# A third tile for the states of the scans, and DRAM rows 36 KB apart

## The chip, the cores and the metric

The kernel runs on one core of one Trainium2 chip. A core has five engines with instruction queues of their own: TensorE (PE, with weight loads PEld beside it) for matmuls, VectorE (DVE) for elementwise work, reductions and scans, ScalarE (ACT) for activation functions and copies, GpSimd (POOL) for elementwise work, and SyncE (SP), which here issues nearly all DMAs. Each engine works through its queue in order; semaphores hold an instruction back until what it needs is there. SBUF is the core's working memory, PSUM the memory that TensorE writes, and DRAM is reached by DMAs, which 16 DMA engines carry out. The metric is the device time of one execution in microseconds.

## The reference, cut to what matters

The input is 16 images of 192 channels on a 32 x 32 grid (L = 1024 positions). Four layers follow each other: an mLSTM block with a 3 x 3 convolution and a batch norm, a channel attention with depthwise convolutions, a two-dimensional selective scan, and a block that mixes rolled copies of the image. The change concerns the third layer (and two small tiles of the second). Its heart, per image, for 4 directions k, 384 channels d and 16 states n:

```python
def step(h, xs_t):
    d_t, u_t, B_t, C_t = xs_t
    dA = jnp.exp(d_t[..., None] * A)
    h = h * dA + (d_t * u_t)[..., None] * B_t[:, :, None, :]
    y = jnp.einsum('bkdn,bkn->bkd', h, C_t)
    return (h, y)
_, ys = jax.lax.scan(step, h0, (dT, uT, BT, CT))
```

The steps d_t are a softplus of a projection of the layer's input; directions 2 and 3 run backwards, and directions 1 and 3 run over the transposed grid.

## The kernel before, in words

All arithmetic is in float32. The first layer runs for all images first, in a loop, and takes about the first 3500 us. Then class `LayersB` does the other three, image by image: `prepare` (second layer and the input side of the third), `scans` (the recurrence), `complete` (the output side of the third layer and the fourth). While image b is scanned, `prepare` of image b+1 and `complete` of image b-1 are woven in.

*Units.* A unit is a scan of one tile of 128 partitions: 16 channels times 8 states, 1024 positions long. Two units (blocks of states 0 to 7 and 8 to 15) make a group, 24 groups a direction, 4 directions an image: 192 units an image, 3072 in all. For each unit:

- ScalarE (`decay`, L1835) makes dA = exp(A x dl) into a ring of three tiles. dl holds the steps of the group's 16 channels, each row repeated on 8 partitions.
- ScalarE (`inputs_up`, L1831), once per group, copies du (step times input, repeated likewise) into one of two PSUM tiles xt.
- VectorE (`inputs`, L1842) multiplies it by the B states bb; both multiplies of a group stand ahead of its two scans.
- VectorE (`scan`, L1851) runs the recurrence over dA and xt into a tile h. There are two h tiles, taken in turn.
- POOL (`outputs`, L1863) multiplies h by the C states cb into hc, a ring of three.
- TensorE (`sums`, L1893) adds over the states with four matmuls into the PSUM tile acc; ScalarE (`collect`, L1903) copies acc out once in four units.

*Steps.* `front` makes the steps of a direction, small pieces at fixed slots: a projection (TensorE), then for each of six halves `ends` (ScalarE: Abs into the tile e, Relu into dlh), `logs` (ScalarE: e = exp(-e), e = ln(1 + e)), and `park` two slots later (L1769; POOL: dlh + e into dlh, dlh times x into duh). `park` stores dlh and duh in the DRAM tiles dld and dud, a row of 1024 positions per channel. Successive halves are six slots apart. `keep` stores the B and C rows in xdr.

*Loads.* `load_group` (L1793) reads 16 rows of dld and of dud, each onto 8 partitions, into a ring of two tiles each; it is issued as soon as the decay that reads the old tile has been put in the queue, three groups ahead. `load_states` (L1789) reads 8 rows of xdr, the whole set 16 times over, into bb and cb. All these go through SP's queue, in which each issue waits its turn.

*Order.* In `scans` the order of all engines' queues is written by the kernel itself, unit by unit (a slot each): decays, scans, products, sums and loads have fixed places, and the pieces of `prepare` and `complete` are put in by `fits` and `advance`, which keep a reckoned clock per engine (constants SLOT, OWN, OVER, LEAST) and ask whether an engine has room before the slot's end. Semaphore waits follow from which instructions touch the same tile. Elementwise and TensorE instructions of the woven-in stages are recorded through one helper and all carry the line L782.

*Small tiles of `prepare`.* kk holds the diagonal of the key products; m1 and m2 hold the two matrices that attention leaves. They lie in a pool of small tiles under the tags m1 and m2. Larger tiles lie in slots that are reused in turn: "pa" (one buffer: x0, later x1) and "w" (two buffers, for weights).

Of the kernel before, what the change touches and what calls it, by code (L numbers as in the profile page):

```python
# [11 lines left out]
F32 = mybir.dt.float32  # L12
# [7 lines left out]
C, H, W = 192, 32, 32  # L20
L = H * W
HL = L // 2
P6 = 96
# [4 lines left out]
K, N, R = 4, 16, 12  # L28
# [13 lines left out]
class Ctx:  # L42
# [22 lines left out]
    def ln_exp(self):  # L65
# [4 lines left out]
        if self.ordered:  # L70
            self.spent["ACT"] += TABLE
        i = self.nc.scalar.preload_act_table_set("natural_log_exp_and_others")
# [672 lines left out]
BLOCKS = N // NBL  # L745
# [10 lines left out]
ENGINES = ("PE", "ACT", "POOL", "DVE")  # L756
ALLOW = {"PE": 2.45, "DVE": 0.3}
OVER = {"PE": (0.8, 1.2), "ACT": (0.0, 1.5), "POOL": (0.5, 1.5)}
LEAST = {"PE": 1.0, "ACT": 0.6, "POOL": 0.8}
TABLE = 1.28  # L760
MARGIN = 0.6


class Metered:


    RATES = {"ACT": (0.07, 0.00105), "POOL": (0.1, 0.0022), "DVE": (0.08, 0.00105), "PE": (0.06, 0.0017)}
    LEAST = {"ACT": 0.2, "POOL": 0.2, "DVE": 0.12, "PE": 0.4}

# [3 lines left out]
    def __getattr__(self, op):  # L773
        f = getattr(self.engine, op)

        def issue(out, *args, **kw):
            base, each = self.RATES[self.name]
            self.spent[self.name] += max(self.LEAST[self.name], base + each * math.prod(out.shape[1:]))
            if op == "activation" and args[1] in (AF.Tanh, AF.Gelu):
                self.spent["ACT"] += TABLE * self.cx.has_ln  # L780
                self.cx.has_ln = False
# [15 lines left out]
class Stream:  # L797
# [16 lines left out]
    def inputs(self):  # L814


        done, engine = self.dones[-3 if self.piped else -1]
        return 0.0 if engine == self.engine else done + MARGIN

# [5 lines left out]
class LayersB:  # L825
# [81 lines left out]
    def setup(self):  # L907

        tc, nc, cx, wp, I, NB = self.tc, self.nc, self.cx, self.wp, self.I, self.NB
        dp = self.dp  # L910
        self.dqd = dp.tile([6, 128, 9, 128], F32, name="dqd")
        self.dvd = dp.tile([2, 2, P6, 9, P6], F32, name="dvd")
        self.vd = dp.tile([P6, 2, L], F32, name="vd")
        self.x0d = dp.tile([P6, 2, L], F32, name="x0d")
        self.x2d = dp.tile([P6, 2, L], F32, name="x2d")
        self.xdr = dp.tile([K, 2 * N, L], F32, name="xdr")
        self.dld = dp.tile([K, 3, 128, L], F32, name="dld")
        self.dud = dp.tile([K, 3, 128, L], F32, name="dud")
        self.xxd = dp.tile([3, 128, L], F32, name="xxd")
        self.yd = dp.tile([3, 128, L], F32, name="yd")  # L920
        self.zd = dp.tile([NB, 3, 128, L], F32, name="zd")
        self.x1d = dp.tile([NB, P6, 2, L], F32, name="x1d")


        bn_g, bn_b = self.vec("bn_g", P6), self.vec("bn_b", P6)
        self.bsc = wp.tile([P6, 2], F32, name="bsc")
        self.bsh = wp.tile([P6, 2], F32, name="bsh")
        with tc.tile_pool(name="b_pre0", bufs=1) as pre:
            st = pre.tile([P6, 2, NB, 12], F32, name="st")
            for a in range(2):  # L930
                nc.scalar.dma_start(
                    st[:, a], self.sdram[:, a * P6 : (a + 1) * P6, :].rearrange("b p s -> p b s")
                )
            mv = pre.tile([P6, 2, 2], F32, name="mv")
            for a in range(2):
                nc.vector.bn_aggr(mv[:, a, :], st[:, a].rearrange("p b s -> p (b s)"))
            sd = pre.tile([P6, 2], F32, name="sd")
            nc.scalar.activation(sd, mv[:, :, 1], AF.Sqrt, bias=cx.eps5[0:P6])
            nc.vector.reciprocal(sd, sd)
            nc.vector.tensor_mul(self.bsc, sd, bn_g)  # L940
            nc.vector.tensor_mul(sd, mv[:, :, 0], self.bsc)
            nc.vector.tensor_sub(self.bsh, bn_b, sd)


        self.offb = wp.tile([P6, P6], F32, name="offb")
        nc.sync.dma_start(self.offb, I["c_off48"])
        self.temp = wp.tile([P6, 2], F32, name="temp")
        for a in range(2):
            for j in range(2):
                nc.sync.dma_start(  # L950
                    self.temp[48 * j : 48 * j + 48, a : a + 1],
                    I["temperature"][2 * a + j : 2 * a + j + 1].unsqueeze(0).to_broadcast([48, 1]),
                )

        self.dw2b = self.vec("dw_b", 128)
        self.pads = [wp.tile([128, H + 2, W + 2], F32, name="pad%d" % i) for i in range(2)]
        for t in self.pads:
            nc.gpsimd.memset(t, 0.0)

        self.xx = wp.tile([128, 3, L], F32, name="xx")  # L960
    def setup_scans(self):

        nc, cx, wp, I = self.nc, self.cx, self.wp, self.I
# [50 lines left out]

        ring = lambda name, n, shape: [wp.tile(shape, F32, name=name + str(i)) for i in range(n)]
        self.y = wp.tile([128, 3, L], F32, name="y")
        self.dA, self.h, self.hc = ring("dA", 3, [128, L]), ring("h", 2, [128, L]), ring("hc", 3, [128, L])
        self.dl, self.du = ring("dl", 2, [128, L]), ring("du", 2, [128, L])
        self.bb, self.cb = ring("bb", BLOCKS, [128, L]), ring("cb", 3, [128, L])
        self.e, self.dlh, self.duh = (wp.tile([128, HL], F32, name=n) for n in ("e", "dlh", "duh"))  # L1020
        self.xd = wp.tile([64 + XR, L], F32, name="xd")
        self.dtw = wp.tile([64 + R, INNER], F32, name="dtw")
        self.xt = [self.xp.tile([128, L], F32, name="xt%d" % i) for i in range(2)]
# [108 lines left out]
    def prepare(self, b):  # L1132

        nc, cx, sm, I = self.be, self.cx, self.sm, self.I
# [42 lines left out]
        for m in range(3):  # L1177
# [5 lines left out]
            elif m == 1:  # L1183
                w1 = self.weight(self.w1d, [P6, 2, C])
            else:
                wpf = self.weight(I["w_projfT"].rearrange("(a p) o -> p a o", p=P6), [P6, 2, C])
# [13 lines left out]

        id6 = cx.ident[0:P6, 0:P6]
        at = sm.tile([P6, 2, P6], F32, tag="at", name="at", bufs=1)
        kk = sm.tile([P6, 2, C], F32, tag="m1", name="kk", bufs=1)[:, :, 0:P6]
        rq = sm.tile([P6, 2], F32, tag="rq", name="rq")
        vs = [self.p4([P6, 2, HL], "vh") for _ in range(2)]
        for hf in range(2):
# [19 lines left out]
        for a in range(2):  # L1226
# [5 lines left out]
                nc, pk[:, ch(a)], [(qT[:, t, k0 : k0 + P6], qT[:, t, k0 : k0 + P6]) for t in range(NCH)]  # L1232
            )
        yield "DVE", 0
        nc.vector.tensor_mul(
            kk, pk.rearrange("p (a c) -> p a c", a=2), id6.unsqueeze(1).to_broadcast([P6, 2, P6])
        )
# [34 lines left out]
        yield "ACT", 0  # L1272
        for a in range(2):
            nc.scalar.mul(at[:, a, :], at[:, a, :], den[:, a : a + 1])
        m1 = sm.tile([P6, 2, C], F32, tag="m1", name="m1", bufs=1)
        m2 = sm.tile([P6, 2, C], F32, tag="m2", name="m2", bufs=1)
        for m_, w_ in ((m1, w1), (m2, wpf)):
            yield "PE", 0
            p = self.mm()[0:P6, 0 : 2 * C]
            for a in range(2):  # L1280
                nc.tensor.matmul(p[:, a * C : (a + 1) * C], lhsT=at[:, a, :], rhs=w_[:, a, :], start=True, stop=True)
            yield "ACT", 0
            nc.scalar.copy(m_, p.rearrange("p (a c) -> p a c", a=2))
        ds = [self.taps(P6, self.dvd[1, 0], I["dw_kv"][ch(0)], b == 0)]
        for hf in range(2):
            for a in range(2):
# [400 lines left out]
    def fits(self, s, end):  # L1687

        if not s.open(self.slots) or s.engine == "SP":
            return s.engine == "SP" and s.open(self.slots)  # L1690
        at = self.clock[s.engine]
        if s.engine != "DVE":
            end += OVER[s.engine][self.slots % BLOCKS]
        wait = s.inputs()
        if wait > at and (s.engine == "DVE" or wait + LEAST[s.engine] > end):
            return False
        return at < end + 0.1 and self.have.get(s.engine, 1.0) > 0.0

# [145 lines left out]
    def scan(self, u):  # L1844
        nc = self.nc
        n, blk = divmod(u, BLOCKS)
        k = n // GROUPS
        views = [self.h[u % 2], self.dA[u % 3], self.xt[(n + 1 + blk) % 2]]
        if k >= 2:
            views = [v[:, ::-1] for v in views]  # L1850
        nc.vector.tensor_tensor_scan(*views, 0.0, op0=ALU.mult, op1=ALU.add)  # L1851

    def outputs(self, u, carried=False):

        n, blk = divmod(u, BLOCKS)

        k = n // GROUPS - K * (carried and u == UNITS - 1)
        views = [self.hc[u % 3], self.h[u % 2], self.c_of(k, blk)]
        if n // GROUPS % 2:
            views = [views[0].rearrange("p (h w) -> p w h", w=W)] + [  # L1860
                v.rearrange("p (w h) -> p w h", h=H) for v in views[1:]
            ]
        self.nc.gpsimd.tensor_mul(*views)  # L1863
# [139 lines left out]
```

## Time and profile before

| what | value |
|---|---|
| median of 3 runs | 15609.16 us (15584.52 to 15626.19) |
| the profiled execution | 15591.93 us, of which the span 15590.1 us |
| busy, share of the span | PE 81%, DVE 79%, POOL 63%, ACT 59% |
| scans, L1851 | 3072 x 2273 ns |
| products with C, L1863 | 3072 x 2371 ns |
| multiplies with B, L1842 | 3072 x 1227 ns |
| decays, L1835 | 3072 x 1146 ns |
| copies of u, L1831 | 1536 x 1014 ns |
| dl and du loads | 2 x 1536 of 512 KB |
| read from DRAM, written | 2018.92 MB, 364.30 MB |

A busy share is the time in which an engine executed something, as a share of the span. A row of the waits view names who waited, for whom, the sum of the idle time, the number of times and the longest. A row of the groups view gives line, engine, operation, tiles, shapes and number, then busy time and mean, then the engine's idle time ahead of these instructions with what ended most of it. The stretches view gives each engine's busy time between two points of the execution, with the clock that TensorE was granted, the busy share of the DMA engines and the rate at which they moved data.

### The profile page before, as it was taken

What the parts mean: (1) busy time and instruction counts of PE and PEld (TensorE: products, weight loads), DVE (VectorE), ACT (ScalarE), POOL (GpSimd) and SP (SyncE); (2) the same over time, 40 slices, a digit from 0 to 9 for tenths busy, and PEclk for the clock granted to TensorE, in tenths of its full rate; (3) what the DMA queues carried; (4) which work ended last, traced back from release to release, by engine and by line L of the source; (5) the groups of instructions that cost most, each with busy time, mean ns of one, the idle gap of its engine ahead of it and who ended that gap; (6) DMA issues with size and microseconds to landing.
All of it is one profiled execution on the core that took longest, in us unless ns stands there. A gap on an engine that the chain in (4) does not pass through costs nothing. (4 is left out here: it accounts for less than half of the span.)

```text
span 15590.1 us, 196674 instructions
## 1 busy us (share of the span) xinstructions
PE 12621.5 (81%) x72384; PEld 5045.6 (32%) x72384; DVE 12310.8 (79%) x10295; ACT 9263.9 (59%) x12084; POOL 9861.8 (63%) x5787
## 2 busy tenths in 40 slices
PE   9999999987787777877787777877787777878755
PEld 5555555542222222222222222222222222222212
DVE  4444444448988999999989898898989898988997
ACT  3333333326666666666666666666666666666665
POOL 1000000006787878787878787878878787878785
PEclk9999999997787888878788888887888887878766
DMA  1000000017777787878787878787777787777775
GB/s 29 12 15 14 15 14 15 15 40 189 201 195 200 188 207 188 210 182 214 182 211 183 213 184 211 183 210 189 202 194 198 194 202 195 199 195 193 201 182 129
DMA packets 852126, 2412.70 MB, mean 155 GB/s; under 512 B 114352, under 2 KB 234240, under 8 KB 843520
## 3 DMA queue, kind: packets, MB, share of 16 engines
q1 hardware_dynamic: 838496, 2397.64, 60.2%
q8 instruction: 580, 9.50, 0.3%
q10 hardware_dynamic: 12704, 2.72, 0.1%
q14 instruction: 346, 2.83, 0.1%
HBM read 2018.92 MB, written 364.30 MB: 153 GB/s over the span
## 5 line engine op out<-in xcount | busy, mean ns | idle before, releaser
L1863 POOL TENSOR_TENSOR hc<-h,cb 128x1024 f32<-128x1024 f32 x3072 | 7247.3, 2371 | 2046.2 <-DVE h L1851 1557.8
L1851 DVE TENSOR_TENSOR_SCAN h<-dA,xt 128x1024 f32<-128x1024 f32 x3072 | 6912.8, 2273 | 297.0 <-POOL hc L1863 289.1
L1842 DVE TENSOR_TENSOR xt<-xt,bb 128x1024 f32<-128x1024 f32 x3072 | 3633.4, 1227 | 852.7 <-ACT xt L1831 718.9
L1835 ACT ACTIVATE dA<-dl,A 128x1024 f32<-128x1024 f32 x3072 | 3506.7, 1146 | 801.2 <-DMA dl<-dld 672.8
L1893 PE MATMUL acc<-hc,sel 128*32 128x256 f32 x24576 | 2406.8, 473 | 1707.6 <-POOL hc L1863 1705.0
L782 PE MATMUL mm<-pad,dg 128*128 128x512 f32 (+1 forms) x5580 | 2899.3, 655 | 13.3 <-ACT pad L782 9.9
L1831 ACT COPY xt<-du 128x1024 f32<-128x1024 f32 x1536 | 1557.6, 1014 | 1361.7 <-DVE h L1851 1183.5
L1893 PEld LDWEIGHTS acc<-hc,sel 128*32 128x32 f32 x24576 | 562.2, 120 | 4055.4 <-POOL hc L1863 2897.2
L782 PEld LDWEIGHTS mm<-pad,dg 128*128 128x128 f32 (+1 forms) x5580 | 995.5, 192 | 1479.2 <-issue 1363.3
L596 POOL TENSOR_TENSOR vw<-va,gtok 128x396 f32<-128x396 f32 x112 | 95.2, 850 | 1712.0 <-ACT va L588 1712.0
L782 PE MATMUL mm<-x,wgt 96*128 96x512 f32 (+1 forms) x1664 | 1064.5, 775 | 140.1 <-ACT o L782 50.0
L1884 PE MATMUL acc<-y,ident 128*128 128x512 f32 x576 | 445.7, 866 | 445.5 <-ACT y L1903 444.5
L782 POOL TENSOR_TENSOR t<-x 96x768 f32<-96x768 f32 (+4 forms) x510 | 647.5, 1290 | 204.6 <-PE mm L782 204.2
L691 POOL TENSOR_TENSOR x_in<-x_in,sz 128x384 f32<-128x384 f32 x128 | 116.8, 913 | 750.5 <-DVE x_in L687 676.7
L782 PE MATMUL mm<-d,xT 128*96 128x256 f32 x2048 | 569.1, 416 | 5.6 <-ACT o L782 5.3
L782 PEld LDWEIGHTS mm<-x,wgt 96*128 96x128 f32 (+1 forms) x1664 | 342.1, 226 | 669.9 <-issue 364.5
L782 POOL TENSOR_TENSOR duh<-dlh,xx 128x512 f32<-128x512 f32 x384 | 537.5, 1400 | 30.1
L782 POOL TENSOR_TENSOR dlh<-dlh,e 128x512 f32<-128x512 f32 x384 | 488.4, 1272 | 103.1 <-ACT e L782 101.2
L782 PE MATMUL mm<-xd,dtw 12*128 12x512 f32 x768 | 534.5, 782 | 10.0 <-ACT z L782 10.0
L622 DVE TENSOR_TENSOR D<-D,s 128x256 f32<-128x256 f32 x768 | 270.8, 415 | 322.6 <-ACT D L619 322.6
L389 PE MATMUL pc<-ypad,w_c 128*64 128x512 f32 (+1 forms) x1152 | 442.9, 633 | 80.4 <-PEq L735 41.3
L619 ACT ACTIVATE D<-s 128x256 f32<-128x256 f32 x768 | 232.7, 390 | 426.3 <-PE s L613 426.3
(331 smaller groups left out, 15374.9 us busy)
## 6 DMA issues: line engine op xcount, KB each, us to landing
dl<-dld SPq DMA_DIRECT2D x1536, 512.0 KB
du<-dud SPq DMA_DIRECT2D x1536, 512.0 KB
dld<-dlh SPq DMA_DIRECT2D x384, 256.0 KB
dud<-duh SPq DMA_DIRECT2D x384, 256.0 KB
bb<-xdr SPq DMA_DIRECT2D x128, 512.0 KB
cb<-xdr SPq DMA_DIRECT2D x128, 512.0 KB
dg<-dqd SPq DMA_DIRECT2D x270, 192.0 KB
zd<-z SPq DMA_DIRECT2D x48, 512.0 KB
```

Of the source, the lines that this page charges most:

```text
L389: nc.tensor.matmul(p[r, :], lhsT=w_, rhs=v, start=(n == 0), stop=(n == 14))
L619: nc.scalar.activation(d, S[j][:, two], AF.Exp)
L622: nc.vector.tensor_mul(d, d, S[j][:, 2 * CH :])
L691: nc.gpsimd.tensor_mul(hT[:, :, cs], hT[:, :, cs], sz[:, :, cs])
L782: return f(out, *args, **kw)
L1831: self.nc.scalar.copy(self.xt[n], self.du[n])
L1835: self.nc.scalar.activation(self.dA[u % 3], self.dl[n % 2], AF.Exp, scale=self.A[:, blk, n : n + 1])
L1842: self.nc.vector.tensor_mul(self.xt[(n + 1 + blk) % 2], self.xt[n % 2], self.bb[blk])
L1851: nc.vector.tensor_tensor_scan(*views, 0.0, op0=ALU.mult, op1=ALU.add)
L1863: self.nc.gpsimd.tensor_mul(*views)
L1884: nc.tensor.matmul(acc, lhsT=self.cx.ident, rhs=self.y[:, g, half(pair)], start=True, stop=False)
L1893: nc.tensor.matmul(self.acc[rows4(q), q4(s)], lhsT=self.sel[:, m, :], rhs=self.hc[u % 3][:, q4(q)], start=False, stop=(s + m + blk == 3),)
```

## The change

The ring of h tiles has three instead of two, and the scan and the product take tile u % 3. The memory comes from three places: the tile e is no longer a tile of its own but another name of duh; kk takes the slot "pa" between x0 and x1; m1 and m2 take buffers of the slot "w". The DRAM tiles xdr, dld and dud get a dimension of 9 of which only place 0 is used, so that their rows, still 4 KB long, lie 36 KB apart. LEAST becomes a pair per engine, read by the slot's block, and both numbers of each pair are the old one.

```diff
-LEAST = {"PE": 1.0, "ACT": 0.6, "POOL": 0.8}
+LEAST = {"PE": (1.0, 1.0), "ACT": (0.6, 0.6), "POOL": (0.8, 0.8)}
+PITCH = 9
...
-        self.xdr = dp.tile([K, 2 * N, L], F32, name="xdr")
-        self.dld = dp.tile([K, 3, 128, L], F32, name="dld")
-        self.dud = dp.tile([K, 3, 128, L], F32, name="dud")
+        self.xdr = dp.tile([K, 2 * N, PITCH, L], F32, name="xdr")[:, :, 0, :]
+        self.dld = dp.tile([K, 3, 128, PITCH, L], F32, name="dld")[:, :, :, 0, :]
+        self.dud = dp.tile([K, 3, 128, PITCH, L], F32, name="dud")[:, :, :, 0, :]
...
-        self.dA, self.h, self.hc = ring("dA", 3, [128, L]), ring("h", 2, [128, L]), ring("hc", 3, [128, L])
+        self.dA, self.h, self.hc = ring("dA", 3, [128, L]), ring("h", 3, [128, L]), ring("hc", 3, [128, L])
...
-        self.e, self.dlh, self.duh = (wp.tile([128, HL], F32, name=n) for n in ("e", "dlh", "duh"))
+        self.dlh, self.duh = (wp.tile([128, HL], F32, name=n) for n in ("dlh", "duh"))
+        self.e = self.duh
...
-        kk = sm.tile([P6, 2, C], F32, tag="m1", name="kk", bufs=1)[:, :, 0:P6]
...
+        kk = self.slot("pa", [P6, 2, P6], "kk")
...
-        m1 = sm.tile([P6, 2, C], F32, tag="m1", name="m1", bufs=1)
-        m2 = sm.tile([P6, 2, C], F32, tag="m2", name="m2", bufs=1)
-        for m_, w_ in ((m1, w1), (m2, wpf)):
+        ms = []
+        for w_ in (w1, wpf):
...
+            m_ = self.slot("w", [P6, 2, C], "m", 2)
+            ms.append(m_)
             nc.scalar.copy(m_, p.rearrange("p (a c) -> p a c", a=2))
+        m1, m2 = ms
...
-        if wait > at and (s.engine == "DVE" or wait + LEAST[s.engine] > end):
+        if wait > at and (s.engine == "DVE" or wait + LEAST[s.engine][self.slots % BLOCKS] > end):
...
-        views = [self.h[u % 2], self.dA[u % 3], self.xt[(n + 1 + blk) % 2]]
+        views = [self.h[u % 3], self.dA[u % 3], self.xt[(n + 1 + blk) % 2]]
...
-        views = [self.hc[u % 3], self.h[u % 2], self.c_of(k, blk)]
+        views = [self.hc[u % 3], self.h[u % 3], self.c_of(k, blk)]
```

## The prediction

> **What bounds the kernel now.** I read the busy shares first, then the stage in which the change works, cut out of the trace, then each engine's waits in that stage. The scans run from about 3530 us to 15460 us; the slices of the page show the busy shares jump there.
>
> The stretches view, with busy time of each engine, then granted clock, DMA share and GB/s. Rows 1 and 2 are the two halves of one plain load (xx, no row read twice; row 2 runs on into a plain store), row 3 is dl, du and cb loads, row 4 a plain y load, and the last row is the whole scan stage:
>
> ```profile
> 7150.40:7153.20 2.80, 2.80 (x13) 0.97 (x12) 2.70 (x4) 1.86 (x2) 2.80 (x4) 0.72 1.02 250
> 7153.40:7157.20 3.80, 3.31 (x18) 1.39 (x17) 3.80 (x2) 0.00 (x0) 3.80 (x5) 1.00 1.02 412
> 5537.20:5541.30 4.10, 4.10 (x19) 1.86 (x18) 4.10 (x2) 1.94 (x2) 4.02 (x4) 1.00 1.00 226
> 5693.00:5694.80 1.80, 1.80 (x12) 0.57 (x11) 1.70 (x2) 1.77 (x3) 1.80 (x1) 1.00 1.01 239
> 3530.00:15460.00 11930.00, 9204.18 (x42540) 3207.12 (x42538) 10738.50 (x7134) 7896.12 (x9521) 9531.36 (x5248) 0.80 0.77 196
> ```
>
> In the last row the columns are PE, PEld, DVE, ACT, POOL. VectorE is busy 10738.5 of 11930 us (90%), POOL 80%, PE 77%, ACT 66%, the DMA engines 77%. VectorE sets the pace: 3072 units at 11930/3072 = 3.88 us each, of which its two large operations take 2.27 + 1.23 us. Only its 1191 us of idle time can be won. The waits view of the scan stage says what ends them (VectorE, then ScalarE; us in total, times, longest):
>
> ```profile
> DVE xt L1842 <- ACT xt L1831: 718.9, 356, 29.7
> DVE h L1851 <- POOL hc L1863: 289.1, 229, 3.3
> ```
>
> ```profile
> ACT xt L1831 <- DVE h L1851: 1183.5, 563, 4.4
> ACT dA L1835 <- DMA dl<-dld: 672.8, 239, 7.7
> ```
>
> The second row is what a third state tile addresses: a scan that cannot start because the product of two units ago still reads its tile. The first is larger, and is ScalarE being late with the copy of u. The last row is one cause of that lateness, a replicated load not yet landed, and is what the row pitch could address. The groups view gives durations:
>
> ```profile
> L1863 POOL TENSOR_TENSOR hc<-h,cb 128x1024 f32<-128x1024 f32 x3072 | 7247.3, 2371 | 2046.2 <-DVE h L1851 1557.8
> L1851 DVE TENSOR_TENSOR_SCAN h<-dA,xt 128x1024 f32<-128x1024 f32 x3072 | 6912.8, 2273 | 297.0 <-POOL hc L1863 289.1
> ```
>
> POOL's 2.37 us fits easily in 3.88, so it is late only when other work sits in front: 1.27 + 1.40 us for the two step products, up to 1.9 us for one roll product. Such a lump is caught up later (POOL itself waits 1557.8 us for scans).
>
> **What the Trainium skill says.** "SBUF — State Buffer", section "SBUF: two separate sides": VectorE and GpSimd share a port pair under an exclusive lock, against a GpSimd read when the VectorE operation has two SBUF inputs. More overlap of scan and product could then stretch both. Here scan and multiply each read one operand from PSUM, and the trace agrees that they are free: the 3072 scans last 2241/2276/2290 ns (least/median/most) with POOL busy 80% of the time. "DMA: Bandwidth & Descriptors", section "Latency and other measured facts", gives row pitches of 512 KiB and more as slow and a few KiB of padding as the cure; neither 4 KB nor 36 KB is such a pitch, so it promises nothing either way, and no run here shows those pitches. The same page's "Where 436 GB/s comes from" puts the ceiling at 435 GB/s; the 412 of row 2 above is near it; row 3, of replicated loads, has 226, and the plain loads of rows 1 and 4 have 250 and 239.
>
> **The change, part by part.**
>
> *Order.* Built, both programs hold the same instructions in the same order on TensorE, VectorE and GpSimd. ScalarE and SP differ only around the first image, before the order is fixed by hand. The pairs in LEAST carry the old values twice. So only waits and addresses change: 0 us from instructions.
>
> *Third h tile.* The scan of unit u now waits for the product of u-3. The longest of the 229 waits is 3.3 us and one unit of slack is 3.88 us, so I count all 289 us as removed at their place. How much stays won? I followed each such wait in the trace to VectorE's next wait for ScalarE. Counting gaps over 50 ns (282 of them, 295 us), for 155 us ScalarE was itself found waiting for VectorE in between, so its work moves forward too and the gain passes. For the other 140 us the late copy comes first, and ScalarE was held by TensorE or a load. These follow VectorE only through the products and decays; I keep 30%, 42 us. Ends: nothing of the 140, or all of it. Taken: 155 + 42 = 197 us, between 155 and 289.
>
> *New lateness.* With three tiles POOL may fall one unit further behind. What is late next is the sum of that unit (L1893), then ScalarE's collect (L1903), once in four units, behind which the next copy of u is queued. 229/4 = 57 cases of 1.26 us is 72 us on ScalarE, which is idle a third of the time; I charge 10 us, 0 to 72.
>
> *e inside duh.* ScalarE's Abs now waits until the previous duh has been stored. In the trace that store lands a median of 4.9 us before the next Abs starts, 0.28 us at the 5th percentile; in the scans 9 are late, by some 4 us together. Behind a late Abs stand the next decay and copy. Cost 4 us; if all 88 cases with under 2 us of room slipped by 2 us, 176 us on ScalarE. What covers it is the three units between one store and the next Abs.
>
> *kk and the m tiles.* kk waits for readers of x0 that are long done. The in_proj weight load must now wait for the attention matmuls just before it, with the next dl and du issues behind it on SP, 15 times. SP there waits for ScalarE's decays anyway (4415 us in its own waits). 5 us, at most 15 x 4 = 60.
>
> *Row pitch.* dl and du rows, and the states' rows, go from 4 KB to 36 KB apart; packets and bytes stay. From the packet records, matched to the issues in order, a 4 KB packet takes 255 ns in a dl load, 280 in du, 261 in cb and 271 in bb, and 159 at best. So there is something to win, but the rows' place does not look like the cause. The patterns have 16 outer steps, and I read them as one step for each of 16 engines: then in cb and bb all engines go through the same eight rows, in dl and du through sixteen different ones, and the times are alike. Plain loads are as slow: y takes 275 ns, x0d 569 for 8 KB against 309 at best. And a dl load that starts on idle queues runs its second to fourth packets per engine at 166 to 206 ns, and the fifth to eighth, of the same rows, at 262 to 324. I take 0 us. Ends: at 159 ns the loads' share of the DMA engines falls from 0.59 to 0.36 and the DMA waits mostly go; of the 719 us, 269 came with ScalarE held by a load within 9 us before (mixed causes included), so up to -269 us. The other end is below as a rival.
>
> **Sum.** -197 + 10 + 4 + 5 = about -180 us against the profiled execution's own 15591.9 us (span 15590.1, 1.8 around it): 15412. The median of the three runs, 15609.2, lies 17 us above that execution, so 15430, 1.2% faster.
>
> **Rivals.**
> 1. *The pitch helps as well.* For it: 672.8 us of load waits, loads at 60% of the best rate. Against: the unreplicated loads just cited. Half to all of 269 us more: 15160 to 15300.
> 2. *The wait only moves.* TensorE is late in the largest group of ScalarE's delays (153 of my count of 411 late copies, 253 us, with nothing else holding ScalarE). If it does not follow VectorE, and POOL's extra lag delays its sums, then only about 40 us stay: 15570, within 0.3%.
> 3. *The pitch hurts, slower.* The replicated loads hold 0.59 of the DMA engines (8 packets per engine x 255 to 280 ns x 3296 loads, 7050 us of 11930), the rest 0.18. Place: load after load behind SP, then the decay L1835. Packets 10% longer land a pair 0.43 us later, 245 x 0.43 = 105 us on ScalarE and 40% of it, 42 us, on VectorE; these grow with new late loads. The gain is spent near packets 1.35 times as long; from (1-0.18)/0.59 = 1.39 times the DMA engines are the bound. At 1.5 times the stage is 11930 x (0.59 x 1.5 + 0.18) = 12700 us: 16380. For it: already 77% busy. Against: nothing shows packets slower on wider rows.
>
> **How the numbers follow.** Forecast 0.50, own range 15350 to 15520. Rival 1: 0.24. Rival 2: 0.14. Rival 3: 0.12. A measurement here tells 0.3% (47 us) from no change. Faster: the first two, with a little given to no change, 0.73; same 0.15; slower 0.12. The range runs from 15120 to 15650: it leaves out rival 3 and the far end of rival 1.
>
> **What would show it.** Right: VectorE's wait for hc at the scan falls from 289 to under 30 us; VectorE's wait for ScalarE's copy grows, by 50 to 130 us; the busy time of VectorE stays within 10 us; dl packets stay at 240 to 270 ns and the load waits at 600 to 800 us. ScalarE's first operation into duh waits under 30 us for the store. The prediction is wrong if the packet times move by more than 10%, or if the copy wait grows by as much as the hc wait falls.

## The result, and the profile after

The changed kernel takes 15568.30 us (median of 19 runs, 15535.38 to 15590.38), the kernel before 15616.94 us (19 runs, 15584.52 to 15640.75). The ratio is 0.9967, 95% interval 0.9959 to 0.9974: 49 us or 0.33% faster. The forecast was 180 us or 1.2%. The result lies in the range, and almost on the 15570 us of the second rival, "the wait only moves", which had a chance of 0.14. The profiled execution of the changed kernel (span 15588.6 us) is the slowest of its 19, so the two spans hide most of the difference: its first scan starts at 3565.0 us, 20 us later than the 3545.2 us of before. The sums of waits below are read for where time sits, and the times of the runs for how much it is.

The page's groups of the changed kernel (busy us, mean ns | idle before it and its releaser; the scan is now L1858, the product L1870, the multiply L1849, the decay L1842):

```profile
L1870 POOL TENSOR_TENSOR hc<-h,cb 128x1024 f32<-128x1024 f32 x3072 | 7241.8, 2371 | 2014.9 <-DVE h L1858 1540.3
L1858 DVE TENSOR_TENSOR_SCAN h<-dA,xt 128x1024 f32<-128x1024 f32 x3072 | 6891.3, 2271 | 43.2 <-POOL hc L1870 43.0
```

Nothing became slower or faster by itself: 2371 and 2271 ns, within 2 ns of before. The scan's idle time went from 297.0 to 43.2 us. The waits view of the scan stage, VectorE and ScalarE of the changed kernel (us in total, times, longest):

```profile
DVE xt L1849 <- ACT xt L1838: 949.2, 414, 33.4
...
DVE h L1858 <- POOL hc L1870: 43.0, 40, 2.0
DVE x L784 <- PE mm L784: 34.3, 21, 2.5
```

```profile
ACT xt L1838 <- DVE h L1858: 1156.3, 550, 4.1
ACT dA L1842 <- DMA dl<-dld: 650.3, 237, 7.9
```

Against the rows of before: the scan's wait for the product fell by 289.1 - 43.0 = 246 us, and the multiply's wait for ScalarE's copy grew by 949.2 - 718.9 = 230 us; the wait of `x` for TensorE, 34.3 us, was 1.6 us before. From the first scan to the last VectorE is idle for 1170 us before and 1177 us after: as long as before, at another instruction. ScalarE's wait for loads of dl is 22 us less. The stretches view has for the scan stage (busy time of PE, PEld, DVE, ACT, POOL, then clock, DMA share and GB/s):

```profile
3530.00:15460.00 11930.00, 9213.52 (x42568) 3209.22 (x42566) 10709.49 (x7134) 7910.14 (x9539) 9531.66 (x5250) 0.80 0.75 196
```

What fell is VectorE's busy time, from 10738.5 to 10709.5 us. By the trace its instructions between the first and the last scan add up to 4 us less than before, and overlap by 25 us more, since a scan that need not wait starts before its neighbour has ended.

**Where the wait went.** The stretch with the longest waits for the product is in the second half of each image. There I set the two kernels side by side in image 6, each from the start of the product of unit 102 (8418.81 us before, 8447.82 us after). The timeline of POOL in the kernel before (start, us, engine, line, operation; in brackets the idle time before it and what ended it):

```profile
8424.83 2.50 POOL L782 TENSOR_TENSOR t<-x 96x512 f32<-96x512 f32 x2 [3.66 <-PE mm L782]
8427.29 4.66 POOL L1863 TENSOR_TENSOR hc<-h,cb 128x1024 f32<-128x1024 f32 x2
8435.61 2.51 POOL L782 TENSOR_TENSOR t<-x 96x512 f32<-96x512 f32 x2 [3.67 <-PE mm L782]
8438.09 2.35 POOL L1863 TENSOR_TENSOR hc<-h,cb 128x1024 f32<-128x1024 f32 x1
```

The same stretch of POOL in the changed kernel:

```profile
8453.84 2.50 POOL L784 TENSOR_TENSOR t<-x 96x512 f32<-96x512 f32 x2 [3.65 <-PE mm L784]
8456.31 4.65 POOL L1870 TENSOR_TENSOR hc<-h,cb 128x1024 f32<-128x1024 f32 x2
8464.63 2.51 POOL L784 TENSOR_TENSOR t<-x 96x512 f32<-96x512 f32 x2 [3.67 <-PE mm L784]
8467.10 2.35 POOL L1870 TENSOR_TENSOR hc<-h,cb 128x1024 f32<-128x1024 f32 x1
```

From their zero points the starts are 6.02, 8.48, 16.80, 19.28 and 6.02, 8.49, 16.81, 19.28 us: POOL's schedule is the same to 0.01 us. It stands still for 3.66 us ahead of `t`, a product of the last stage's rolled images, and it waits there for TensorE, not for VectorE. `t` lies in a ring of three tiles (`c4`, which three other tiles of `complete` use too), and the tile is free when TensorE's matmuls with `row` have read it. What TensorE does meanwhile, in the changed kernel:

```profile
8453.43 1.04 PE L1900 MATMUL acc<-hc,sel 128*32 128x256 f32 x8
8458.70 1.08 PE L1900 MATMUL acc<-hc,sel 128*32 128x256 f32 x8 [4.23 <-POOL hc L1870]
8459.71 3.73 PE L784 MATMUL mm<-vf,m 96*96 96x512 f32 x4
8463.37 1.08 PE L784 MATMUL mm<-t,row 96*32 96x256 f32 x8
```

The sums stand in TensorE's queue ahead of the matmuls that read `t`, and wait 4.23 us for POOL's product hc. POOL's product stands in its queue behind `t`, which waits for those matmuls. This is a loop of two engines, each waiting for the other once a turn. One turn is 8464.63 - 8453.84 = 10.79 us for two units, and adds up from its rows: 8464.63 - 8458.70 = 5.93 us from the sum to the freed tile, 2.5 us of `t`, 2.35 us of hc. VectorE is in no part of it.

The clock has a part in it. These are TensorE's 5.93 us in the changed kernel, and the same four matmuls of `vf` with `m` in the run *t_ring4* described below (last three numbers: clock, DMA share, GB/s):

```profile
8458.70:8464.63 5.93, 5.93 (x21) 1.61 (x22) 3.42 (x3) 4.75 (x5) 2.26 (x1) 0.50 0.28 68
8359.01:8360.97 1.96, 1.96 (x8) 0.64 (x12) 1.96 (x1) 1.96 (x3) 1.96 (x2) 1.00 0.00 0
```

At a granted clock of 0.50 the four matmuls take 3.73 us, at 1.00 they take 1.96 us, and the eight with `row` take 1.08 and 0.64 us. An estimate from these: at 1.00 throughout, the sum taken to shrink like the eight with `row`, a turn would last 10.79 - 1.77 - 2 x 0.44 = 8.1 us for two units, near the mean pace of 2 x 3.88 us. In the kernel before, 44 of POOL's 90 waits of this kind, 150 of 204 us, come behind 4 us with a mean clock of at most 0.55. So the ring of three is short mainly where TensorE is at half clock; no run changes the clock by itself.

What a third h tile does to VectorE there is seen in its own timeline. Before:

```profile
8429.66 2.29 DVE L1851 TENSOR_TENSOR_SCAN h<-dA,xt 128x1024 f32<-128x1024 f32 x1 [3.27 <-POOL hc L1863]
8440.47 2.29 DVE L1851 TENSOR_TENSOR_SCAN h<-dA,xt 128x1024 f32<-128x1024 f32 x1 [3.29 <-POOL hc L1863]
```

and after:

```profile
8458.68 2.29 DVE L1858 TENSOR_TENSOR_SCAN h<-dA,xt 128x1024 f32<-128x1024 f32 x1 [0.65 <-POOL hc L1870]
8463.48 0.68 DVE L784 TENSOR_TENSOR x<-x,mm 96x512 f32<-96x512 f32 x1 [2.51 <-PE mm L784]
8464.08 2.27 DVE L1858 TENSOR_TENSOR_SCAN h<-dA,xt 128x1024 f32<-128x1024 f32 x1
8469.49 2.29 DVE L1858 TENSOR_TENSOR_SCAN h<-dA,xt 128x1024 f32<-128x1024 f32 x1 [0.67 <-POOL hc L1870]
```

The waiting scans lie 10.81 us apart in both kernels. The changed one is a unit ahead, and instead of one wait of 3.27 us it has 0.65 us for the product and 2.51 us for a result of TensorE: 3.16 us. Here the tile bought one unit of lead, once, and not a faster turn.

### The profile page after: what moved, and what is told of

The parts are those of the page before. It is cut to its first block, busy times and chain, and to the rows that moved or that the text cites. A ratio compares the mean times of both kernels' runs of the same rounds, so it can differ in the third digit from the quotient of the medians.

```text
span 15588.6 us, 196212 instructions
## 1 busy us (share of the span) xinstructions
PE 12639.1 (81%) x72384; PEld 5058.7 (32%) x72384; DVE 12282.4 (79%) x10295; ACT 9264.5 (59%) x12084; POOL 9858.2 (63%) x5787
## 4 chain that ended last, share of the span: by engine, by line
PE 19%; DVE 17%; POOL 13%; issue 13%; DMA 10%; ACT 8%; SPq 1%; DVEq 0%; ACTq 0%; POOLq 0%
PE mm L784 14%; DVE h L1858 10%; POOL hc L1870 9%; DVE xt L1849 5%; DMA du<-dud 3%; DMA dl<-dld 3%; PE acc L1900 3%; ACT xt L1838 2%; ACT dA L1842 2%; POOL t L784 2%; DMA yh<-yd 1%; POOL dlh L784 1%; PE acc L1891 1%; DMA y<-ydram 1%; POOL duh L784 1%
## 5 line engine op out<-in xcount | busy, mean ns | idle before, releaser
L1870 POOL TENSOR_TENSOR hc<-h,cb 128x1024 f32<-128x1024 f32 x3072 | 7241.8, 2371 | 2014.9 <-DVE h L1858 1540.3
L1858 DVE TENSOR_TENSOR_SCAN h<-dA,xt 128x1024 f32<-128x1024 f32 x3072 | 6891.3, 2271 | 43.2 <-POOL hc L1870 43.0
L1849 DVE TENSOR_TENSOR xt<-xt,bb 128x1024 f32<-128x1024 f32 x3072 | 3633.4, 1227 | 1074.1 <-ACT xt L1838 949.2
L1842 ACT ACTIVATE dA<-dl,A 128x1024 f32<-128x1024 f32 x3072 | 3506.7, 1146 | 718.6 <-DMA dl<-dld 650.3
L784 POOL TENSOR_TENSOR t<-x 96x768 f32<-96x768 f32 (+4 forms) x510 | 647.9, 1291 | 205.6 <-PE mm L784 169.9
L784 POOL TENSOR_TENSOR dlh<-dlh,duh 128x512 f32<-128x512 f32 x384 | 488.9, 1273 | 112.5 <-ACT duh L784 112.3
```

Of the source, the lines that this page charges most:

```text
L784: return f(out, *args, **kw)
L1842: self.nc.scalar.activation(self.dA[u % 3], self.dl[n % 2], AF.Exp, scale=self.A[:, blk, n : n + 1])
L1849: self.nc.vector.tensor_mul(self.xt[(n + 1 + blk) % 2], self.xt[n % 2], self.bb[blk])
```

## The experiments

Eleven kernels were run in three groups, and each group shares its runs of the kernel before. The theories are spelled out in the expectations.

**The parts one by one.** *ring_only* is the changed kernel with rows 4 KB apart:

```diff
-PITCH = 9
+PITCH = 1
```

> Three h tiles and the shared memory, DRAM rows 4 KB apart as before. Theory A (VectorE does not set the pace where it waited for hc; a loop of POOL and TensorE does): the wait for hc falls from 289 to about 43 us, the wait for ScalarE's copy grows by 180 to 250 us, and the time is 0.998 to 1.000 of before. Theory B (the ring is worth what was forecast, and the pitch gives most of it back): 0.987 to 0.990. Theory C (the shared memory gives it back): the time is that of the changed kernel or above, and the run with sharing alone is 1.005 or more.

Measured 15584.19 us, 0.9984 of before (0.9976 to 0.9993). VectorE waits 955.6 us for the copy and 42.7 us for the product, as in the whole change and as theory A has it.

*pitch_only* is the kernel before with the rows apart, `xdr`, `dld` and `dud` as in the change and nothing else.

> Two h tiles and memory as before, DRAM rows 36 KB apart. Theory A: the packets of dl and du get 1 to 3% shorter as in the changed kernel (252 and 272 ns instead of 255 and 280), and the time is 0.997 to 0.999 of before: the rest of the change's 0.33%. Theory B: 1.006 to 1.010. Theory C: 1.000.

Measured 15600.02 us, 0.9990 (0.9984 to 0.9997): 11 us. By the packet records a packet takes 255 ns in a dl load and 270 in a du load, where the kernel before had 255 and 280, and 86 ns in the store of du, where it had 93. The rows' distance helps a little, and for du more than for dl; the time is at the edge of theory A's band.

*share_only* is the changed kernel without ring and pitch: what is left is e inside duh, and kk, m1 and m2 in slots.

```diff
-PITCH = 9
+PITCH = 1
...
-ring("h", 3, [128, L])
+ring("h", 2, [128, L])
```

With the number of h tiles the index changes, u % 2 for u % 3, here and in the runs below.

> The shared memory alone (e under the name of duh, kk and the m tiles in slots), two h tiles, rows 4 KB apart. Theories A and B: 0.999 to 1.001 of before. Theory C: 1.005 to 1.010.

Measured 15612.44 us, 1.0005 (0.9996 to 1.0013): no difference, which rules out theory C. So the ring by itself is 15612.44 - 15584.19 = 28 us, of a wait of 282.1 us in share_only that became 42.7: 12% of what was removed. The tighter sequence seen above, some 25 us of overlap, is of this size, so next to nothing is left for the removed wait itself. The three parts together give 28 + 11 - 1 = 38 us, and the whole change measured 49 us (40 to 64 by its interval); the runs don't tell whether the rest is interaction.

**The loop.** *t_ring4* is the changed kernel with two h tiles again, and the 4 KB given to a fourth tile in the ring of `t`. The order of the instructions on TensorE, VectorE and GpSimd is that of the changed kernel.

```diff
-        return self.slot("c4", shape, name, 3)
+        return self.slot("c4", shape, name, 4)
...
-ring("h", 3, [128, L])
+ring("h", 2, [128, L])
```

> The changed kernel with two h tiles instead of three, and in their place a fourth tile in the ring c4, which the roll products t on POOL use. Theory A (POOL, held in front of a roll product until TensorE has read the product of three before, is what makes hc late): POOL's wait for TensorE in front of t falls from 204 us to under 80, VectorE's wait for hc from 289 to under 180, and the time is 0.990 to 0.997 of before. Theory B (VectorE's own waits decide): without the third h tile the wait for hc stays at 250 to 290 us and the time is within 0.002 of that with the pitch alone.

Measured 15420.27 us, 0.9872 (0.9855 to 0.9889): 191 us faster than before, of which row pitch and sharing account for about 10; theory A's band began at 0.990, and the gain is larger. It beats both kernels and computes all that they do. The waits view of its scan stage, VectorE:

```profile
DVE xt L1849 <- ACT xt L1838: 726.2, 356, 34.2
DVE h L1858 <- POOL hc L1870: 104.3, 161, 2.9
```

With two h tiles the scan's wait for the product fell from 289 to 104 us, and here the copy's wait did not grow (718.9 before, 726.2 now). POOL's wait of `t` for TensorE, 204.2 us in 90 times before and 169.9 us in 84 in the changed kernel, is gone from the list. POOL's timeline at the same units of image 6:

```profile
8351.10 2.35 POOL L1870 TENSOR_TENSOR hc<-h,cb 128x1024 f32<-128x1024 f32 x1 [3.96 <-DVE h L1858]
8353.41 2.51 POOL L784 TENSOR_TENSOR t<-x 96x640 f32<-96x640 f32 x2
8355.88 2.37 POOL L1870 TENSOR_TENSOR hc<-h,cb 128x1024 f32<-128x1024 f32 x1
8358.52 2.38 POOL L1870 TENSOR_TENSOR hc<-h,cb 128x1024 f32<-128x1024 f32 x1 [0.28 <-DVE h L1858]
8360.85 1.29 POOL L784 TENSOR_TENSOR t<-x 96x512 f32<-96x512 f32 x1
```

`t` starts at once (the last row is cut off by the window), and POOL waits for VectorE, as one wants it. From the product of unit 102 to that of unit 108 there pass 22.28 us (8358.52 to 8380.80), against 28.98 before and 28.79 in the changed kernel. From the first scan to the last the stage is 176 us shorter than before (11729.5 against 11906.0 us), and VectorE is idle 172 us less. So the loop of GpSimd and TensorE is shown as the cause of most of the scan's wait, and not only inferred from the trace. The granted clock is higher too, 0.847 in the mean of the runs against 0.840, and 0.69 against 0.62 over these six units; what part of the gain came with it is not separated. But at half clock `t` doesn't wait here either: at 8366.74 us the four matmuls with `m` take 3.73 us as before, and the next `t` starts at 8368.27 us, straight behind hc.

*t4_d5* adds a fifth tile to another ring, of four, between GpSimd and TensorE in the last stage (a second line of that ring is changed likewise):

```diff
-self.slot("d3", [128, 2, CH], "d3", 4)
+self.slot("d3", [128, 2, CH], "d3", 5)
```

> The run with four roll tiles (two h tiles, rows 36 KB apart), and a fifth tile in the ring d3 of the diagonal products on POOL, which waited some 81 us for TensorE there. Theory A (POOL held in front of a woven-in product by TensorE delays the products with C): a further 20 to 60 us, 0.983 to 0.986 of before. Theory B: no change to the run with four roll tiles, 0.987.

Measured 15424.55 us, 0.9885 (0.9868 to 0.9901), the same as t_ring4: theory B. POOL's wait for TensorE at this ring's tile `d` fell from 82.6 to 10.7 us, and its wait for scans grew from 1591.0 to 1654.3 us. This ring limits nothing, although POOL waited in it.

**The ring of h once the loop is wider.** *t4_h2* and *t4_h3* both have four tiles for `t`, and two or three for h. Both don't fit into SBUF together with everything else, so two weight tiles are left out in both, and their skip term and x_proj projection are computed with other weights. The first pair of lines is what sets the two apart, the second is in both:

```diff
-ring("h", 2, [128, L])
+ring("h", 3, [128, L])
...
-lhsT=self.dskip[:, g, rows4(2 * pair + i)],
+lhsT=self.cx.ident[:, rows4(2 * pair + i)],
```

> The kernel with four tiles in the ring of the roll products and two tiles of states, with the two weight tiles dskip and xpj left out to make room (the identity and the columns of perm are read in their place, so the skip term and the x_proj projection use other weights; the shapes of all instructions stay). It is the control for the next run. Both theories: within 15 us of 15420, VectorE's wait for the product at the scan 90 to 120 us, for the copy of u 700 to 750 us.

> As the control, but with three tiles of states: the change's ring in a kernel where the loop of GpSimd and TensorE has been widened (dskip and xpj are left out here too). Theory A, what is left of the scan's wait is still the mark of a slower neighbour: the wait goes, the copy wait takes up most of it, and the third tile is worth 0 to 30 us against the control. Theory B, without that loop the wait is VectorE's own: 80 to 105 us faster than the control, and the copy wait stays within 30 us.

The control measured 15409.62 us (15397.95 to 15413.30), 0.9869 (0.9854 to 0.9884); with three tiles 15340.67 us (15339.29 to 15371.44), 0.9830 (0.9817 to 0.9844). The control is where both theories put it. The runs of the two don't overlap; the medians lie 69 us apart (four and five runs; the means 60 us). The waits view, VectorE, of the control and then of the three tiles:

```profile
DVE xt L1839 <- ACT xt L1828: 723.3, 351, 33.6
DVE h L1848 <- POOL hc L1860: 104.0, 163, 3.0
```

```profile
DVE xt L1839 <- ACT xt L1828: 791.3, 381, 33.5
```

The scan's wait is gone altogether (0.2 us), and the copy's grew by 68 us. The runs lie between the two theories, outside the band of either: the time is nearer to B, the copy's wait is what A said. As with the change itself, a part of the gain is busy time: in the window VectorE is busy 10778.0 us in the control and 10746.4 us with three tiles. From the first scan to the last the stage is 61 us shorter in the two profiles, 32 us of it busy and 30 us idle time. So the same edit is worth 28 us where 240 us of wait went, nearly all of it overlap, and 69 us where 104 us went. Of the wait itself, the part that came from the loop returned next to nothing, and of the rest some 30 of 104 us were won.

**Is VectorE the bound?** Each filler is an operation on 128 x 2 elements, put into the changed kernel once a unit, in the queue of one engine. *fill_dve* puts it behind the scan:

```diff
+nc.vector.tensor_scalar(self.fil, self.fil, 1.0, None, op0=ALU.mult)
```

> The changed kernel with one small operation on VectorE (128x2, about 0.14 us, 3072 times, some 430 us of work) after each scan. Theory A (the pace is shared; VectorE sets it only in part of the stage): each us of work costs 0.4 to 0.75 us, 1.010 to 1.018 of before. Theory B (VectorE sets the pace through the scan stage): 0.9 to 1.0 us for each, 1.021 to 1.025.

Measured 16249.98 us, 1.0408 (1.0389 to 1.0427). The group's row of the changed kernel with this filler (busy us, mean ns):

```profile
L1861 DVE TENSOR_SCALAR fil<-fil 128x2 f32<-128x2 f32 x3072 | 1633.4, 532 | 0.0
```

It is no small operation: 532 ns in the mean, as it is held by GpSimd's work, which the last section shows. 1633 us on VectorE cost 16249.98 - 15568.30 = 682 us, 0.42 us for each: theory A's price for each us, at a time outside both bands. The granted clock was lower, too, 0.829 against 0.840. An engine that sets the pace would have given nearly one.

*fill_dve_rec* repeats it with an operation that keeps short:

```diff
+nc.vector.reciprocal(self.fil, self.fil)
```

> The changed kernel with a reciprocal of 128x2 on VectorE after each of the 3072 scans, some 0.15 us each and 460 us in all. Theory A, VectorE is not the bound for about half of the time: 0.3 to 0.6 us of time per us of filler, 140 to 280 us over the changed kernel, as the other filler gave 0.42. Theory B, VectorE sets the pace: 0.85 to 1.0, 390 to 460 us. Of the filler itself: if the earlier one was held because it shares a port with GpSimd in a faster mode, these all last under 0.3 us; if any small VectorE operation is held by GpSimd, hundreds of them last over 0.4 us again.

Measured 15605.44 us, 0.9997 (0.9988 to 1.0005): 37 us over the changed kernel.

```profile
L1861 DVE RECIPROCAL fil<-fil 128x2 f32<-128x2 f32 x3072 | 424.1, 138 | 0.0
```

That is 37 / 424 = 0.09 us for each us of filler, below theory A's band, and far from the 0.85 to 1.0 of theory B. Not all of the 424 us is new busy time, because neighbours on VectorE overlap at their ends: in the scan stage VectorE's busy time went from 10709.5 to 10890.2 us, 181 us. Even of those only 37 / 181 = 0.2 reached the end; counted in the same way, fill_dve's 682 us are 0.52 of 1316 us (VectorE's busy time in the whole execution, 13598.7 against 12282.4 us). What took the rest: the copy's wait is 852.5 us here, 97 less than without the filler.

*fill_pool* and *fill_act* put one behind the product and one behind the decay:

```diff
+self.nc.gpsimd.tensor_scalar(self.fil, self.fil, 1.0, None, op0=ALU.mult)
...
+self.nc.scalar.mul(self.fil, self.fil, 1.0)
```

> The changed kernel with one small operation on POOL (128x2, about 0.21 us, 3072 times, some 640 us of work) after each product with C. Theory A: POOL sets the pace where the roll products stand, so each us costs 0.2 to 0.5 us, 1.005 to 1.018 of before. Theory B: POOL, 80% busy, takes it in its idle time, under 0.1 us for each, below 1.002.

> The changed kernel with one small operation on ScalarE (128x2, about 0.2 us, 3072 times, some 615 us of work) after each decay. Theory A: the copies of u come later, each us costs 0.3 to 0.7 us, 1.009 to 1.025 of before. Theory B: ScalarE, 66% busy, takes it in its idle time, under 0.1 us for each, below 1.002.

On GpSimd, 15653.34 us, 1.0034 (1.0020 to 1.0049): 663.7 us of filler cost 85 us, 0.13 for each, which is between the bands and settles little. On ScalarE, 15590.50 us, 0.9985 (0.9977 to 0.9992): 582.6 us cost 22 us, 0.04 for each, as theory B has it. The fillers ran in other groups than the changed kernel; measured through the kernel before of each group, the four costs are 690, 44, 93 and 31 us, which changes no reading. So the time of none of these three engines alone is the bound in this kernel: VectorE's price is 0.09 to 0.42, GpSimd's 0.13, ScalarE's 0.04. I did not fill TensorE, and its clock, by the trace, is part of the loop.

## Why the prediction was wrong

**The opening, "VectorE sets the pace".** It was read from 90% busy in the scan stage. The fillers contradict it: 0.09 and 0.42 us for each us put on VectorE. "Only its 1191 us of idle time can be won" missed that busy time can fall too, by 29 us here, which is the size of the ring's whole gain. And what ends the idle time was taken from the releaser's name. The releaser of a scan is POOL's product, and the question that was not put is what POOL was doing. The same waits view has, for POOL and TensorE of the kernel before:

```profile
POOL t L782 <- PE mm L782: 204.2, 90, 4.8
```

```profile
PE acc L1893 <- POOL hc L1863: 1705.0, 989, 7.7
```

Each waits for the other. The prediction read POOL's lateness as a lump that "is caught up later"; in the loop it is not caught up, it is repeated every 10.8 us.

**"Third h tile", the step that failed.** All 289 us were counted as removed at their place; 246 went, nearly right. Kept were 155 + 42 = 197 us; the ring alone measured 28 (ring_only against share_only), and most of the wait came back as a longer wait for the copy, 230 us. The 155 us were those waits where ScalarE was itself found waiting for VectorE in between, which I took for proof that the gain passes on. It proves only that ScalarE waited for VectorE then, not that it would be done earlier. With the loop a VectorE that is one unit ahead meets TensorE's and ScalarE's results at the times at which they came before, as the 0.65 + 2.51 us in place of 3.27 show. The lower end of this term, 155 us, was no bound, because the mechanism behind it was wrong and not its size.

**"New lateness", 10 us.** Not measured by itself; it is inside the 28.

**"e inside duh" and "kk and the m tiles", 9 us together.** share_only: +1 us, with an interval from -6 to +20. Right that they cost next to nothing.

**"Row pitch", 0 us.** pitch_only: 11 us faster (5 to 25). Small as taken, but not nothing: packets of du went from 280 to 270 ns. Neither rival 1 (packets towards 159 ns) nor rival 3 (packets 1.35 times as long) came near. The prediction read the Trainium skill's row on pitches a little too widely: in "DMA: Bandwidth & Descriptors", section "Latency and other measured facts", a pitch of 512 KiB still has 207 GB/s, with 214 as the full rate, and the fall to 164 and 103 comes at 2 and 4 MiB. No run here has such a pitch.

**Rival 2, "the wait only moves".** Its 15570 us is the result, and its reason was half right: where the loop runs, TensorE doesn't follow VectorE. That TensorE and GpSimd hold each other through a ring of three tiles was not in it. That the number fits so well is luck in part: it allowed 40 us for the ring, which gave 28, and nothing for the pitch, which gave 11, and it started from 15609 us, where the longer series has 15617.

**What was to show it.** The wait for the product at 43 us, where under 30 was said; the copy's wait +230 us, where 50 to 130 was said; that is the stated sign of a wrong prediction ("as much as the hc wait falls"), and it was there. VectorE's busy time moved by 29 us, not under 10. dl packets at 252 ns and load waits of 650.3 us are inside what was said, and ScalarE waited 1.1 us for the store ahead of its operations into duh, where under 30 was said. No packet time moved by more than 10%.

## What to carry to other kernels

Before pricing a buffer that ends a wait, look at what the releasing engine was waiting for just then, and follow this until the chain either comes back to the waiting engine or closes without it. If it closes without it, the wait is a symptom: another tile for the waiting engine buys its depth once, and the same 4 KB in the ring inside the loop bought 191 us here against 49. Such a wait is a reason to try a tile there, not a proof: with a fifth tile the ring of `d` lost 72 us of wait, and no time was won. A high busy share doesn't say that an engine sets the pace; a short filler in its queue tests it, and its own duration has to be read before it is believed.

## What the runs showed of the hardware

A `tensor_scalar` of 128 x 2 elements on VectorE, from SBUF to SBUF in float32, is held while GpSimd works. Of the 3072 in fill_dve 1364 began while GpSimd was idle, and none of these lasted over 151 ns. The other 1708 began inside a GpSimd operation, and all but one lasted until that operation ended (to within 40 ns) or longer. 657 lasted over 0.4 us, 1122 us together, and each of these ended within 33 ns of the end of a GpSimd operation. The longest, in VectorE's timeline:

```profile
13399.90 7.46 DVE L1861 TENSOR_SCALAR fil<-fil 128x2 f32<-128x2 f32 x1
13407.27 2.35 DVE L1851 TENSOR_TENSOR xt<-xt,bb 128x1024 f32<-128x1024 f32 x2
```

and GpSimd's at that time:

```profile
13397.73 2.52 POOL L784 TENSOR_TENSOR t<-x 96x768 f32<-96x768 f32 x2
13400.21 4.69 POOL L1873 TENSOR_TENSOR hc<-h,cb 128x1024 f32<-128x1024 f32 x2
13404.86 2.47 POOL L784 TENSOR_TENSOR t<-x 96x768 f32<-96x768 f32 x2
```

It starts behind a scan, while GpSimd is in `t`, and comes free at 13407.36 us, with the end of the last `t` (13407.33 us): operation after operation on GpSimd went ahead of it. The Trainium skill says that VectorE in a mode that uses two ports, and GpSimd, take a shared port pair by an exclusive lock, and that the loser blocks ("SBUF — State Buffer", section "SBUF: two separate sides"), and it lists `tensor_scalar` of float32 in SBUF among the operations with a 2x mode ("VectorE: DVE Perf Modes", section "The perf-mode tier table (the rule you actually need)"). The trace agrees, and it shows that a hold can last longer than one operation: the page gives the pair for one whole instruction, and the filler above waited out the rest of one and four more. The other filler fits too: none of the 3072 reciprocals lasted over 145 ns (130/139/145, least, median, most), though 1970 of them began inside a GpSimd operation. The mode itself is nowhere recorded, so that the mode is what makes the difference remains argued. The scans and multiplies of this kernel, with one operand in PSUM, show no such hold: their means in fill_dve are 2274 and 1222 ns.
